# The last two of 32 expert steps behind a branch on the planned number of steps

## The chip, the cores and the metric

The kernel runs on one core of a Trainium2 chip. A core has a matmul engine (TensorE, "PE" in the profile), a vector engine (VectorE, "DVE"), an activation engine (ScalarE, "ACT"), GpSimd ("POOL") and SyncE ("SP"). Each engine works through its own list of instructions in order, and semaphores tie the lists together. DMA queues carry data between DRAM and the on-chip memory; here SP and ACT issue the plain transfers, and POOL the ones whose addresses are read from a table. The metric is device microseconds (us) of a whole execution of the kernel, as the median of several runs.

## What is computed

Two layers of a graph network over 3125 nodes of 256 features. Each layer adds a graph part and a linear attention part to `x`, and then a mixture of experts. The change touches the experts of layer 0, which in the reference are these lines (cut):

```python
N, E, D, H = 3125, 8, 256, 1024
logits = xt @ Wr + br
top_p, top_idx = jax.lax.top_k(jax.nn.softmax(logits, axis=-1), 2)
weights = top_p / top_p.sum(axis=-1, keepdims=True)
xn = (xt - mu) * jax.lax.rsqrt(var + LN_EPS)
xe = xn[None] * ln_g[:, None, :] + ln_b[:, None, :]
h = jax.nn.gelu(jnp.einsum('end,edh->enh', xe, W1) + b1[:, None, :], approximate=False)
y = jnp.einsum('enh,ehd->end', h, W2) + b2[:, None, :]
out = (weights[:, :, None] * y_of_the_two_chosen_experts).sum(axis=1)
```

Each of the 3125 tokens uses two of the 8 experts, so there are 6250 token-expert pairs; which expert gets how many depends on the data.

## The kernel before, in words

**Stages.** `fast` runs, one after the other: counting the edges and layer 0's graph and attention parts; the routing of the tokens; layer 0's experts; the projections for layer 1 (the loop over `NB` = 25 tiles of 128 nodes that begins with the gather of L2342); and layer 1 itself. `gps_two_layers` ends with a branch (L2418): if a flag is set, a slower general program follows; otherwise its code is skipped.

**Routing.** `Routes.tokens` computes the router, picks two experts per token, and scatters the normalized tokens (POOL, L1947) to the DRAM table `route_x`, where each expert has a region of 13 tiles of `TS` = 256 rows. `Routes.clear` writes zeros to all of that table beforehand, 256 rows per DMA on SP, dealt out at four DMAs per load of `at` in the loop over layer 0's node groups. `Routes.plan` counts the tiles. Every expert's first tile is always run, which makes 8 steps (`NE0`). The further tiles of expert e, max(ceil(count/256) - 1, 0) of them, are numbered through by a running sum `cum` (L1965), so that `cum[7]` is the number of further steps that the data need. There can be at most `NT` = (2 * 3125) // 256 = 24 of those, and the kernel always runs all 24. `tiles` holds expert and first row of each; the steps beyond `cum[7]` get some valid tile that nobody asked for, and what they write is read by nobody.

**Experts.** `experts` runs 8 + 24 = 32 steps. A step loads (SP) 256 rows of tokens, small vectors and the expert's two weight matrices, 1 MB each; step s loads for s + 1 ahead, with two buffers of weights. From step 8 on, SP reads expert and row from `tiles` into registers. Then for each of 8 pieces of the hidden layer: two matmuls (L2068, `fhp`) and a gelu on ACT (L2069, `fhid`); the transposes of the next step's tokens (L2051, `ftp`) and their scaling on DVE (L2053, `fxe`); 16 matmuls with W2 (L2076, `fyp`), a DVE addition (L2078, `fy`), and a store of 256 rows to the DRAM table `route_y` (ACT, L2079). Under `manual_schedule` PE, DVE and ACT keep the order in which the code is written; SP and POOL do not.

**Beside the experts.** `beside(s)` puts pieces of another job, the edge lists for layer 1 (`B_.finish`), between the steps: one piece after each step from step 8 on. After the last step it runs what is left of them, which ends with the matmuls `b_ep` (L1125), a chain of small DVE operations (L1128 to L1140) and the store `b_rows` (SP, L1141), and then the check sum `tot` (L2298).

**After the experts.** The pools of the experts' buffers are given back. SP loads layer 1's weights: `wq`, `wo` (L353, 256 KB each), `wt` (L353, 2 MB), `wkv` (L2321, twice 256 KB) and small ones. POOL gathers for every tile of nodes two tiles `y` from `route_y` (L2342), DVE adds them to `xs` (L2345) and normalizes, PE transposes (L345) and multiplies with `wt` (L2362, `hp`).

Of the kernel before, what the change touches and what calls it, by code (L numbers as in the profile page):

```python
# [10 lines left out]
I32 = mybir.dt.int32  # L11
AF = mybir.ActivationFunctionType
OP = mybir.AluOpType
AX = mybir.AxisListType
PSUM = bass.MemoryType.PSUM
# [3 lines left out]
P = 128  # L19
# [14 lines left out]
NE0, H0 = 8, 1024  # L34
# [872 lines left out]
BIG = 1e30  # L907
RW = 7
MIXED = 8
CW = 8  # L910
GB = 4
TOGETHER = [(0, 4), (4, 4), (8, 4), (12, 4), (16, 4), (20, 3), (23, 2)]
GROUPS1 = GROUPS[:5] + [(2560, 256), (2816, 256), (3072, 128)]
TS = 256
# [229 lines left out]
class Layer1:  # L1144
# [66 lines left out]
    def turn(self, A, c):  # L1211

        if c >= A["n"]:
            return
        k = min(CW, A["w"] - c * CW) * P
        ot = self.wk.tile([P, CW * P], BF, name="ot", bufs=3)
        self.nc.vector.tensor_scalar(ot[:, :k], A["oe"].pop(c)[:, :k], self.C.p, None, op0=OP.is_equal)
        A["ot"][c] = ot
# [610 lines left out]
class Routes:  # L1829


    def __init__(self, nc, C, pool, dram):
        t = lambda shape, dt, name: pool.tile(shape, dt, name=name)
        self.x = dram.tile([NE0 * XR, D], F32, name="route_x")
        self.y = dram.tile([(NE0 + NT) * TS, D], F32, name="route_y")
        self.slot = t([P, 2, NB], I32, "slot")
        self.at = t([P, 2, NB], F32, "route_at")
        self.ex = t([P, 2, NB], F32, "route_ex")
        self.more = t([P, NE0], F32, "route_more")
        self.cum = t([P, NE0], F32, "route_cum")  # L1840
        self.wt = t([P, 2, NB], F32, "route_w")
        self.start = t([P, NE0], F32, "route_start")
        nc.vector.tensor_scalar(self.start, C.row[:, :NE0], float(XR), None, op0=OP.mult)
        self.down = t([P, NE0], F32, "route_down")
        nc.vector.tensor_scalar(self.down, C.row[:, :NE0], -1.0, float(NE0), op0=OP.mult, op1=OP.add)
        self.base = t([P, NE0], F32, "route_base")
        nc.vector.tensor_copy(self.base, self.start)
        self.ones = t([P, P], F32, "route_ones")
        nc.vector.memset(self.ones, 1.0)
        self.tiles = t([1, 2, NT], I32, "route_tiles")  # L1850

    def clear(self, tc, z):

        for i in range(0, NE0 * XR, 2 * P):
            tc.keep_in_program_order(
                tc.nc.sync.dma_start(self.x[i:i + 2 * P, :].rearrange("(p a) d -> p (a d)", p=P), z))
            yield

    def tokens(self, tc, C, wk, ps, xs, t0, nt, wr, br):
# [93 lines left out]
    def plan(self, nc, C, wk):  # L1953


        t = lambda shape, name, dt=F32: wk.tile(shape, dt, name="pl_" + name, bufs=1)
        cnt = t([P, NE0], "cnt")
        nc.vector.tensor_tensor(cnt, self.base, self.start, OP.subtract)
        ci = t([P, NE0], "ci", I32)
        nc.vector.tensor_scalar(ci, cnt, float(-TS), 0.0, op0=OP.add, op1=OP.max)  # L1960
        nc.vector.tensor_single_scalar(ci, ci, TS - 1, op=OP.add)
        nc.vector.tensor_single_scalar(ci, ci, 8, op=OP.arith_shift_right)
        more, cum = self.more, self.cum
        nc.vector.tensor_copy(more, ci)
        nc.vector.tensor_tensor_scan(cum, self.ones[:, :NE0], more, 0.0, op0=OP.mult, op1=OP.add)  # L1965
        sh = [1, NT, NE0]
        le = t(sh, "le")
        nc.vector.tensor_tensor(le, cum[0:1, None, :].to_broadcast(sh),
                                C.row[0:1, :NT, None].to_broadcast(sh), OP.is_le)
        ex = t([1, NT], "ex")  # L1970
        nc.vector.tensor_reduce(ex, le, AX.X, OP.add)
        nc.vector.tensor_tensor(le, le, more[0:1, None, :].to_broadcast(sh), OP.mult)
        done = t([1, NT], "done")
        nc.vector.tensor_reduce(done, le, AX.X, OP.add)

        nc.vector.tensor_tensor(done, C.row[0:1, :NT], done, OP.subtract)
        nc.vector.tensor_scalar(done, done, 1.0, float(XR // TS - 1), op0=OP.add, op1=OP.min)
        nc.vector.tensor_scalar(ex, ex, float(NE0 - 1), None, op0=OP.min)
        nc.vector.tensor_copy(self.tiles[:, 0, :], ex)
        row = t([1, NT], "row")  # L1980
        nc.vector.tensor_scalar(row, ex, float(XR // TS), None, op0=OP.mult)
        nc.vector.tensor_tensor(row, row, done, OP.add)
        nc.vector.tensor_scalar(self.tiles[:, 1, :], row, float(TS), None, op0=OP.mult)
# [25 lines left out]
        nc.vector.tensor_copy(self.back, rank)  # L2009


def experts(tc, C, T, a, pool, wp, wk, ps, beside):

    nc = tc.nc
    K1 = H0 // P

    def fetch(s):
        if s < NE0:
            e, row = s, s * XR
            we = lambda w: w[e:e + 1]  # L2020
            col = lambda v: v[:, e:e + 1, :]
        else:
            ld = lambda i, hi: nc.values_load(
                T.tiles[0:1, i, s - NE0:s - NE0 + 1], engines=[SPE], min_val=0, max_val=hi,
                skip_runtime_bounds_check_because="a step of the plan")
            e, row = ld(0, NE0 - 1), ld(1, NE0 * XR - TS)
            we = lambda w: w[bass.ds(e, 1)]
            col = lambda v: v[:, bass.ds(e, 1), :]
        x = wk.tile([P, TS // P, D], F32, name="fx")
        rows = T.x[row:row + TS, :] if s < NE0 else T.x[bass.ds(row, TS), :]  # L2030
        nc.sync.dma_start(x, rows.rearrange("(t p) d -> p t d", p=P))
        lng, lnb = (wk.tile([P, 1, 2], F32, name=f"fln{c}") for c in "gb")
        b1 = wk.tile([P, 1, K1], F32, name="fb1")
        b2 = wk.tile([P, D], F32, name="fb2")
        nc.sync.dma_start(lng, col(a["L0_ffn_ln_gc"]))
        nc.sync.dma_start(lnb, col(a["L0_ffn_ln_bc"]))
        nc.sync.dma_start(b1, col(a["L0_ffn_b1c"]))
        nc.sync.dma_start(b2, we(a["L0_ffn_b2"]).to_broadcast([P, D]))
        w1 = wp.tile([P, 2, H0], F32, name="fw1")
        nc.sync.dma_start(w1, we(a["L0_ffn_W1"]).rearrange("e (k p) n -> p (e k) n", p=P))  # L2040
        w2 = wp.tile([P, K1, D], F32, name="fw2")
        nc.sync.dma_start(w2, we(a["L0_ffn_W2"]).rearrange("e (k p) n -> p (e k) n", p=P))
        return x, w1, w2, lng, lnb, b1, b2

    def turn(got):
        x, lng, lnb = got[0], got[3], got[4]
        xe = wk.tile([P, 2, TS], F32, name="fxe")
        tp = ps.tile([P, 2, TS], F32, name="ftp", bufs=1)
        for k in range(2):
            for t in range(TS // P):  # L2050
                nc.tensor.transpose(tp[:, k, t * P:(t + 1) * P], x[:, t, k * P:(k + 1) * P], C.id)  # L2051
        for k in range(2):
            nc.vector.tensor_scalar(xe[:, k, :], tp[:, k, :], lng[:, 0, k:k + 1], lnb[:, 0, k:k + 1],  # L2053
                                    op0=OP.mult, op1=OP.add)
        return xe

    steps = NE0 + NT
    got = [fetch(0)]
    xe = turn(got[0])
    for s in range(steps):  # L2060
        if s + 1 < steps:
            got.append(fetch(s + 1))
        x, w1, w2, lng, lnb, b1, b2 = got[s]
        hid = wk.tile([P, K1, TS], F32, name="fhid")
        for i in range(K1):
            hp = ps.tile([P, TS], F32, name="fhp")
            for k in range(2):
                nc.tensor.matmul(hp, w1[:, k, i * P:(i + 1) * P], xe[:, k, :], start=(k == 0), stop=(k == 1))  # L2068
            nc.scalar.activation(hid[:, i, :], hp, AF.Gelu, bias=b1[:, 0, i:i + 1])  # L2069
        if s + 1 < steps:  # L2070
            xe = turn(got[s + 1])
        y = wk.tile([P, TS // P, D], F32, name="fy")
        for t in range(TS // P):
            yp = ps.tile([P, D], F32, name="fyp")
            for i in range(K1):
                nc.tensor.matmul(yp, hid[:, i, t * P:(t + 1) * P], w2[:, i, :], start=(i == 0),  # L2076
                                 stop=(i == K1 - 1))
            nc.vector.tensor_tensor(y[:, t, :], yp, b2, OP.add)  # L2078
        nc.scalar.dma_start(T.y[s * TS:(s + 1) * TS, :].rearrange("(t p) d -> p t d", p=P), y)  # L2079
        beside(s)  # L2080
# [32 lines left out]
def fast(ctx: ExitStack, tc: tile.TileContext, a, out, flag):  # L2113
# [155 lines left out]
    with tc.tile_pool(name="blk", bufs=1) as blk, tc.tile_pool(name="blk_p", bufs=1, space=PSUM) as blk_p, \  # L2269
# [8 lines left out]
        def beside(s):  # L2278
# [9 lines left out]
                    next(loads, None)  # L2288
            else:
                next(steps, None)  # L2290
            if s < NE0 + NT - 1:
                return
            run_all(steps)

# [8 lines left out]
        with tc.tile_pool(name="fw", bufs=2) as fw, tc.tile_pool(name="fk", bufs=3) as fk, \  # L2303
                tc.tile_pool(name="fp", bufs=2, space=PSUM) as fp:
            with tc.manual_schedule(engines=ORDERED):
                experts(tc, C, T_, a, f, fw, fk, fp, beside)


    with tc.tile_pool(name="n1", bufs=1) as n1:
# [161 lines left out]
```

## Time and profile before

| what | us |
|---|---|
| runs shown: median (lowest to highest, 3 runs) | 3045.12 (3043.67 to 3058.38) |
| the profiled execution, its own time | 3573.77 |
| its span on the core | 3571.6 |
| PE busy in it | 2645.9 (74%) |
| DVE busy in it | 1843.1 (52%) |
| POOL busy in it | 990.8 (28%) |
| granted PE clock, mean of the span | 0.864 |
| stage of layer 0's experts (first to last matmul L2051/L2076) | 928 to 1415 |

The profiled execution is one execution under the hardware profiler; it took 529 us longer than the median of the runs shown. All positions ("at 1415") are us from the start of its span. In the rows, "PE L2076 MATMUL fyp<-fw,fhid ... x32" means line 2076, operation, tile written and tiles read, and how often. A matmul of 32-bit numbers is two instructions in the trace, so the 8 x 2 matmuls of a step's first half are 32. SPq and ACTq rows are transfers being issued, not transferred. "[10.36 <-DMA wkv...]" is the idle time of the engine before the row and what the profiler took to have ended it.

### The profile page before, as it was taken

The page shows a single profiled execution, that of the slowest core. Times are in us where ns is not written, and L with a number is a line of the kernel's source. Part 1 is how long each engine was busy: PE and PEld are TensorE (multiplying, and loading weights), DVE is VectorE, ACT ScalarE, POOL GpSimd, SP SyncE. Part 2 cuts the span into 40 slices and gives each one's busy share as a digit, 9 for nine tenths or more (in the row PEclk, how much of TensorE's full clock was granted, in tenths as well). Part 3 has the DMA queues.
Part 4 walks back from the last instruction along what each step waited for, and adds up shares of the span by engine and source line. Part 5 has one row for each costly group of instructions (what it writes and reads, how often), then busy time and mean ns, then how long its engine had stood idle before and what let it go on. Part 6 is the DMA issues. An engine that isn't in the chain of part 4 may idle for free.

```text
span 3571.6 us, 38056 instructions
## 1 busy us (share of the span) xinstructions
PE 2645.9 (74%) x13443; PEld 1791.6 (50%) x13485; DVE 1843.1 (52%) x4089; ACT 741.6 (21%) x1662; POOL 990.8 (28%) x1040
## 2 busy tenths in 40 slices
PE   3787999999699998899053557757656747756778
PEld 2555545546588887444043434534444534444456
DVE  7997977565311111866145444545545454454452
ACT  3443111222222222322001011111101111111122
POOL 1000000012360000400634553354444534544500
PEclk9999999999799999899576777778877878877889
DMA  3333565332566655533423333243333433343312
GB/s 98 81 73 88 164 211 165 99 104 74 160 201 203 196 161 175 156 126 128 128 79 83 97 110 103 81 114 104 106 98 101 117 90 92 100 121 87 107 57 84
DMA packets 388220, 421.79 MB, mean 118 GB/s; under 512 B 144181, under 2 KB 322618, under 8 KB 387764
## 3 DMA queue, kind: packets, MB, share of 16 engines
q1 hardware_dynamic: 317486, 270.75, 25.3%
q0 software_dynamic: 49072, 132.49, 13.4%
q10 hardware_dynamic: 21462, 16.03, 1.5%
q8 instruction: 108, 1.77, 0.2%
q14 instruction: 92, 0.75, 0.1%
HBM read 321.17 MB, written 97.96 MB: 117 GB/s over the span
## 4 chain that ended last, share of the span: by engine, by line
PE 50%; DVE 18%; another core or an unknown queue 17%; issue 6%; DMA 5%; ACT 3%; POOL 1%; ACTq 1%; SPq 0%; DVEq 0%; POOLq 0%
PE agg L2218 8%; PE fyp L2076 6%; PE fhp L2068 6%; PE sums L1492 6%; PE hp L1284 5%; PE hp L2362 4%; PE yp L1336 3%; DVE r L1478 2%; DVE oh_a L1656 2%; PE hp L2240 1%; DVE oh_s L1656 1%; DMA at<-adj 1%; PE kv L1764 1%; PE cnt L1671 1%
## 5 line engine op out<-in xcount | busy, mean ns | idle before, releaser
L1403 POOL DMA_INDIRECT r<-tab,b_at x831 | 795.4, 957 | 1101.5 <-ACT xt L1550 447.2
L1492 PE MATMUL sums<-r,oh 128*128 128x264 f32 x1662 | 459.3, 434 | 99.5 <-DVE oh L1481 41.3
L1492 PEld LDWEIGHTS sums<-r,oh 128*128 128x128 f32 x1662 | 355.8, 217 | 194.9 <-issue 87.9
L1228 PE MATMUL dp<-a,ot 128*128 128x64 bf16 x2493 | 118.1, 211 | 351.6 <-DVE own L1239 128.2
L1239 DVE TENSOR_TENSOR own<-dp,orel 128x512 f32<-128x512 f32 (+1 forms) x122 | 74.2, 608 | 490.6 <-remote 338.1
L1228 PEld LDWEIGHTS <-ot 128*128 128x128 bf16 x2493 | 109.2, 110 | 382.8 <-issue 202.1
L1947 POOL DMA_INDIRECT route_x<-x,slot x50 | 50.6, 1012 | 819.7 <-DVE slot L1943 646.3
L1478 DVE TENSOR_TENSOR r<-r,fixed 128x1792 f32<-128x1792 f32 (+2 forms) x123 | 239.5, 1947 | 3.4 <-ACT fixed L1466 3.4
L2068 PE MATMUL fhp<-fxe,fw 128*128 128x256 f32 x1024 | 234.0, 386 | 8.3 <-ACT fhid L2069 7.6
L1336 PE MATMUL yp<-ew,h 128*128 128x256 f32 x600 | 174.4, 443 | 85.6 <-DVE xs L1340 68.7
L1287 ACT ACTIVATE h<-hp,bc 128x512 f32<-128x512 f32 (+2 forms) x168 | 104.9, 639 | 635.5 <-remote 312.6
L2076 PE MATMUL fyp<-fw,fhid 128*128 128x256 f32 x1024 | 226.3, 379 | 0.0
L2218 PE MATMUL agg<-at,py 128*128 128x512 bf16 (+5 forms) x1181 | 215.1, 333 | 2.6 <-issue 1.8
L2218 PE MATMUL agg<-at,px 128*128 128x512 bf16 (+2 forms) x1027 | 213.9, 356 | 1.2 <-DMA row_b<-in_L_gnn_b 0.2
L2068 PEld LDWEIGHTS fhp<-fxe,fw 128*128 128x128 f32 x1024 | 186.9, 192 | 49.4 <-ACT fhid L2069 15.5
L1284 PE MATMUL hp<-xt,ew 128*128 128x512 f32 (+2 forms) x336 | 183.5, 677 | 30.0 <-ACT h L1287 24.6
L2076 PEld LDWEIGHTS fyp<-fw,fhid 128*128 128x128 f32 x1024 | 192.1, 190 | 24.8
L2362 PE MATMUL hp<-wt,xt 128*128 128x512 f32 x400 | 184.6, 610 | 11.1 <-issue 4.4
L1336 PEld LDWEIGHTS yp<-ew,h 128*128 128x128 f32 x600 | 128.7, 223 | 124.8 <-DVE xs L1340 75.1
L2069 ACT ACTIVATE fhid<-fhp,fb 128x256 f32<-128x256 f32 x256 | 120.6, 474 | 299.1 <-PE fhp L2068 221.0
L1284 PE MATMUL hp<-h,ew 128*128 128x512 f32 (+2 forms) x336 | 158.6, 599 | 0.0
L2342 POOL DMA_INDIRECT y<-route_y,slot x50 | 50.7, 1014 | 384.6 <-DMA wq<-in_L_mix_wqT 350.2
(422 smaller groups left out, 3843.7 us busy)
## 6 DMA issues: line engine op xcount, KB each, us to landing
fw<-in_L_ffn_W SPq DMA_DIRECT2D x64, 1024.0 KB
ew<-in_L_ffn_expert_w SPq DMA_DIRECT2D x126, 256.0 KB
at<-adj SPq DMA_DIRECT2D x44, 640.0 KB
route_x<-zero SPq DMA_DIRECT2D x104, 256.0 KB
tab<-stage SPq DMA_DIRECT2D x25, 1056.0 KB
oe<-b_order SPq DMA_DIRECT2D x97, 256.0 KB
adj<-adj_o SPq DMA_DIRECT2D x78, 250.0 KB
r<-tab,b_at POOLq DMA_INDIRECT x831
```

Of the source, the lines that this page charges most:

```text
L1228: nc.tensor.matmul(dp[:, i, :, :].rearrange("p h r -> p (h r)"), ot[:, i * P:(i + 1) * P], A["a3"][:, j, :], start=(j == 0), stop=(j == 2))
L1284: nc.tensor.matmul(hp[:, :W], ws[i, e][:, n, j * P:(j + 1) * P], x[:, n, :W], start=(n == 0), stop=(n == 1))
L1336: nc.tensor.matmul(yp, h2[e][:, n, i * P:(i + 1) * P], ws[3, e][:, n, :], start=(n == 0), stop=(n == 1))
L1403: st = self.nc.gpsimd.indirect_dma_start(out=r[:, c, :], out_offset=None, in_=self.table, in_offset=bass.IndirectOffsetOnAxis(ap=self.B.at ...
L1478: nc.vector.tensor_tensor(rv, rv, self.factors[:, s0:s0 + k, :, None].to_broadcast([P, k, HD, DH]), OP.mult)
L1492: mm = nc.tensor.matmul(self.sums, oh[:, c, :], r[:, c, :], start=(i == 0), stop=(i == w - 1))
L1656: nc.vector.tensor_tensor(oh.rearrange("p w (m two) -> p w m two", two=2), self.row, v[:, :, None, :].to_broadcast(self.shape), OP.is_equal)
L2068: nc.tensor.matmul(hp, w1[:, k, i * P:(i + 1) * P], xe[:, k, :], start=(k == 0), stop=(k == 1))
L2069: nc.scalar.activation(hid[:, i, :], hp, AF.Gelu, bias=b1[:, 0, i:i + 1])
L2076: nc.tensor.matmul(yp, hid[:, i, t * P:(t + 1) * P], w2[:, i, :], start=(i == 0), stop=(i == K1 - 1))
L2218: nc.tensor.matmul(agg[g][:, :cw], parts[j][:n, k, g * P:(g + 1) * P], at[:n, i, :cw], start=(k == 0 and j == 0), stop=(k == NB - 1 and j ...
L2362: nc.tensor.matmul(hp.rearrange("p r d -> p (r d)"), xt[:, k, :], wt[:, k, j * 512:(j + 1) * 512], start=(k == 0), stop=(k == 1))
```

## The change

The number of further steps, compared with 22, is kept on the chip as `over`. The first 30 steps run as before; the last two run inside `tc.If(over > 0)`, as a call of `experts` of its own with its own buffers, which loads the first of its two steps itself. The rest of `beside`'s job, which was run after step 31, is run after step 29. Since the rows of `route_y` that steps 30 and 31 would write may now stay unwritten, `clear` writes zeros to them too. In the diff, line numbers count lines of the file before and after.

```diff
+SELDOM = 2
@@ class Routes
+        self.over = t([1, 1], I32, "route_over")
@@ def clear
-        for i in range(0, NE0 * XR, 2 * P):
+        pieces = [(self.x, i) for i in range(0, NE0 * XR, 2 * P)]
+        pieces += [(self.y, i * TS) for i in range(NE0 + NT - SELDOM, NE0 + NT)]
+        for x, i in pieces:
             tc.keep_in_program_order(
-                tc.nc.sync.dma_start(self.x[i:i + 2 * P, :].rearrange("(p a) d -> p (a d)", p=P), z))
+                tc.nc.sync.dma_start(x[i:i + 2 * P, :].rearrange("(p a) d -> p (a d)", p=P), z))
@@ def plan
         nc.vector.tensor_tensor_scan(cum, self.ones[:, :NE0], more, 0.0, op0=OP.mult, op1=OP.add)
+        nc.vector.tensor_single_scalar(self.over, cum[0:1, NE0 - 1:], float(NT - SELDOM), op=OP.is_gt)
@@ def experts
-def experts(tc, C, T, a, pool, wp, wk, ps, beside):
+def experts(tc, C, T, a, pool, wp, wk, ps, beside, first, steps):
-    steps = NE0 + NT
-    got = [fetch(0)]
-    xe = turn(got[0])
-    for s in range(steps):
+    got = {first: fetch(first)}
+    xe = turn(got[first])
+    for s in range(first, steps):
@@ def fast: beside
-            if s < NE0 + NT - 1:
+            if s < NE0 + NT - SELDOM - 1:
                 return
             run_all(steps)
@@ def fast
-                experts(tc, C, T_, a, f, fw, fk, fp, beside)
+                experts(tc, C, T_, a, f, fw, fk, fp, beside, 0, NE0 + NT - SELDOM)
+        with tc.If(nc.values_load(T_.over[0:1, 0:1], min_val=0, max_val=1) > 0):
+            with tc.tile_pool(name="fw_l", bufs=2) as fw, tc.tile_pool(name="fk_l", bufs=3) as fk, \
+                    tc.tile_pool(name="fp_l", bufs=2, space=PSUM) as fp:
+                with tc.manual_schedule(engines=ORDERED):
+                    experts(tc, C, T_, a, f, fw, fk, fp, lambda s: None, NE0 + NT - SELDOM, NE0 + NT)
```

## Prediction, written before the result

> **What bounds the kernel now.** I read three views, from coarse to fine. First the busy times by stretch: the experts' stage, then the gap behind it, then layer 1's projections. (Columns: stretch, length, busy time and count of PE, PE weight load, DVE, ACT, POOL, granted clock, DMA share, GB/s.)
>
> ```profile
> 1330.00:1415.00 85.00, 85.00 (x404) 72.45 (x402) 12.62 (x40) 22.78 (x48) 0.00 (x0) 1.00 0.55 161
> 1415.00:1435.00 20.00, 1.36 (x9) 0.86 (x8) 7.27 (x26) 2.54 (x6) 11.54 (x12) 0.57 0.76 256
> 1435.00:1515.00 80.00, 71.38 (x189) 33.75 (x190) 66.42 (x203) 23.34 (x67) 39.17 (x38) 0.89 0.53 163
> ```
>
> In the last steps PE is busy 85.00 of 85.00 us at granted clock 1.00: each us of matmul there is a us of the kernel. In the next 20 us PE does next to nothing. So two prices are wanted: of two steps, and of the gap. For both, the chain that ended last (start, length, what):
>
> ```profile
> 1386.68 0.22 PE b_ep L1125 x2
> 1386.90 6.93 PE fhp L2068 x32
> 1393.82 0.44 PE ftp L2051 x4
> 1394.26 6.91 PE fyp L2076 x32
> 1401.17 6.96 PE fhp L2068 x32
> 1408.13 6.92 PE fyp L2076 x32
> 1415.08 0.42 DVE fy L2078
> ...
> 1417.45 9.40 DMA wkv<-in_L_mix_wkT
> 1426.85 0.49 DVE xs L2345
> ```
>
> Steps 30 and 31 follow each other on PE without a hole; then the chain leaves PE for transfers. The timeline of the gap:
>
> ```profile
> 1403.94 0.32 SPq L1141 DMA_DIRECT2D b_rows<-b_add  x1
> 1415.53 0.37 ACTq L2079 DMA_DIRECT2D route_y<-fy  x1
> 1415.94 0.38 SPq L353 DMA_DIRECT2D wq<-in_L_mix_wqT  x1
> 1418.50 1.02 POOL L2342 DMA_INDIRECT y<-route_y,slot  x1 [350.16 <-DMA wq<-in_L_mix_wqT]
> 1426.85 0.48 DVE L2345 SCALAR_TENSOR_TENSOR xs<-y,route_w,xs 128x256 f32<-128x256 f32 x1 [10.36 <-DMA wkv<-in_L_mix_wkT]
> 1433.82 1.09 PE L345 MATMUL tp<-ident,x 128*128 128x128 f32 x4 [17.91 <-DVE x L338]
> 1435.06 8.79 PE L2362 MATMUL hp<-wt,xt 128*128 128x512 f32 x16
> ```
>
> The gather names `wq` as what it waited for, but it reads `route_y`: the last store, issued until 1415.90, is its likely cause, so a 256 KB store lands within 2.6 us. Likewise the first `xs` needs the gathers, not `wkv`: they were issued 2.6 us behind 3 MB of weights and share the DMA engines with them. POOL idled 350 us before; nothing runs past this gap, so whatever the stage saves arrives at the end.
>
> **Is the branch taken?** No row tells. I ran the reference's routing on its own inputs: the experts get 779, 1053, 1364, 1084, 120, 330, 1129 and 391 tokens, so 3+4+5+4+0+1+4+1 = 22 further steps. 22 > 22 is false: the steps are skipped. It would need 122 more tokens on one expert (391 to 513) to make it 23; rounding can't do that.
>
> **What goes.** By the chain, from 1386.68 to 1415.05: 0.22 + 14.28 + 13.88 = 28.4 us. Step 29 also loses the transposes for step 30, 0.44 us on PE. Of the 28.4, `b_ep` (0.22) only moves behind step 29. With T0 as the end of the last `fyp`, T0 comes **28.8 us earlier**. ACT's 16 gelus, four `fy`, and the loads of two steps on SP (4 MB of weights) go with it and gain nothing: they ran under PE.
>
> **What comes, early.** `over` is one DVE operation of about 0.17 us (as its neighbour L1965) in the plan at 918; the next matmul waits for `fx` until 928, so nothing. SP reads `over` ahead of the first `fx` load (in the changed program it stands just before it); that load waited for the scatters until 925.27, seven us after `over` is there: nothing; without that cover about 0.5 us. The two zeroings of `route_y` are two more SP issues of 0.6 us and 512 KB at about 600, at the end of layer 0's graph part, where the `at` loads run four buffers ahead and PE waits for none: nothing, at most 1.2 us.
>
> **What comes, at the branch.** Every engine reads `over`, compares and jumps. The rows show SP reading registers in the steps: between `fw` at 1358.10 (0.38 long) and `fx` at 1359.00 one read cost 0.52 us; between `fx` and `flng` (1360.35) 0.98. I take 0.5 for the three engines with work there; they read side by side. The skipped stretch costs something too: the changed program has, for the path not taken, a place where SP waits for all transfers on the eight hardware DMA semaphores before it counts on. Queued behind it are the `wq` to `wkv` loads, and POOL's first gather, which needs those counts. Times from T0:
>
> - before: `fy` done +0.45, `wq` issued +0.9, first gather +3.45, first `xs` +11.8, first `hp` +20.0.
> - after: the job beside ends here, uncovered: DVE's chain from `b_et` to `b_add` (1401.55 to 1403.65 in the trace, 2.1 us) follows `fy`, to +2.6; `b_rows` is issued +2.9 to +3.2 (0.29 behind, as in the trace) and lands 2.6 later at most: +5.8. Then the gather, +6.1 instead of +3.45. SP also reads the other flag now before `wq` (0.5 to 1.0): +6.9 instead of +0.9.
>
> So the gather is 2.65 us late and the weights 6.0. But the gathers now stand ahead of the weights. Unhindered, the first lands at 6.1 + 0.95 + 2.6 = +9.7, and by the trace 7.0 us of DVE and 1.2 of transposes follow: `hp` could start at +17.9. It needs `wt` as well: 2.5 MB up to `wt`, with 0.8 MB of gathers in between, at the 0.36 MB/us of that stretch, is 9.1 us: about +18 with the latency. The bounds: 2.1 us gained (+17.9), or 6.0 lost (all of SP's delay on the path, +26). The weights were just in time before, the gathers late; nearest to that row is no great change. I take +21, a loss of **1.0 us**.
>
> **A rule against the change.** "Runtime: NRT & Kernel Launch", section Instruction fetch mechanics, says a taken branch breaks the sequential prefetch, and that a target outside the window held on chip stalls the engine for a fetch. It gives no price. The skipped body is 272 instructions on PE (136 matmuls, each with a weight load) but some 33 on SP, 18 on ACT, 8 on DVE, none on POOL. The nearest row is the branch at the kernel's end over the whole general program: the last output is issued until 3565.69, the span ends at 3571.6, so that jump, the last write and the closing cost 5.9 us together. By the row at its worst, a stall on SP would put `wq` at +12.8 and `hp` up to +32: 12 lost. By the rule read closely, only PE's jump is long, and PE has 17.9 us of idleness to hide it. I take nothing and keep the 12 as a rival.
>
> **After the branch.** The order of instructions differs a little in the first and last of the 25 projection tiles: DVE and ACT operations of neighbouring tiles swapped. That stage keeps PE 71 and DVE 66 of 80 us; I allow 3 us either way and take nothing.
>
> **Sum.** 3573.8 - 28.8 + 1.0 = 3546.0 for the profiled execution. It took 529 us more than the median, and nothing shows where. The steps are matmuls back to back at full granted clock, which an ordinary run cannot shorten, so I subtract the same 27.8: 3045.1 - 27.8 = **3017.3 us**.
>
> **Rivals.**
> - The branch is dear (12 lost as above): gain 16.8, 3028. For it: the whole gap hangs on SP's list. Against: its jump is short.
> - Ordinary runs spend less on the steps, by the ratio 3045/3574: gain 24.5 - 1.0, 3021.6. For it: the unexplained 529 us. Against: clock 1.00 and PE without a hole.
> - Slower: the branch is taken, deciding from a count of 23. Then step 30's loads start only at +3.2 instead of a step ahead: six issues with register reads (about 0.6 each) up to `w1`, 1.4 MB at 0.36 MB/us is 3.9, 2.6 of latency, and 1.7 of transposes and scaling: the first `fhp` at about +13.5 instead of at once, plus 0.5 for the reads: 3059. For it: the count sits on the very edge. Against: the 122 tokens.
>
> **Numbers.** Likeliest case 0.76, dear branch 0.10, cheaper steps 0.08, taken 0.04, the rest unforeseen. The likeliest case's own ends are gains of 28.8 + 2.1 + 3 = 33.9 and 28.8 - 6.0 - 3 = 19.8. The runs before scatter from -1.5 to +13 about their median, so I take 3009 to 3029. 0.5% of 3045 is 15.2 us, about what a measurement can tell from no change: faster means below 3029.9. Faster 0.88 (all of the first and third case and some of the dear branch), same 0.07, slower 0.05.
>
> **What would show it.** Right: 960 `fhp` and `fyp` matmuls instead of 1024, 30 stores of `route_y`, 60 loads of `fw`; the last `fyp` ending near 1386.2; `b_rows` some 3 us later; the first gather near 1392.3, the first `hp` near 1407; a span near 3544. Wrong: 1024 `fhp` with a hole of 13 us in them (taken); the first gather more than 9 us behind the last `fyp` (SP's wait or a fetch); a projection stage longer than 80 us by more than 3.

## The result and the profile after

| | us |
|---|---|
| before, median (lowest to highest, 5 runs) | 3057.8 (3043.7 to 3059.7) |
| after, median (lowest to highest, 5 runs) | 3027.1 (3005.5 to 3033.0) |
| after / before, 95% interval | 0.9899 (0.9876 to 0.9921) |
| the gain by that ratio, of 3057.8 | 30.9 (24 to 38) |
| span of after's profiled execution | 3025.3 |

The changed kernel is faster by 1.0%, with an interval that leaves out 1; the forecast was 3017.3, its range 3009 to 3029, its gain 27.8. The three runs of before that the prediction started from had a median of 3045.1; with two more it is 3057.8.

Lines of the changed kernel are those of its own file: `fhp` L2068 is now L2072, `ftp` L2051 L2056, `fyp` L2076 L2080, `b_ep` L1125 L1126, `b_rows` L1141 L1142, `wkv` L2321 L2330, the gather L2342 L2351, `xs` L2345 L2354, `hp` L2362 L2371; the branch is L2311.

Groups and DMA issues on the page of the changed kernel:

```profile
L2072 PE MATMUL fhp<-fxe,fw 128*128 128x256 f32 x960 | 219.5, 387 | 0.9 <-DVE fxe L2058 0.6
L2080 PE MATMUL fyp<-fw,fhid 128*128 128x256 f32 x960 | 212.2, 379 | 0.0
...
fw<-in_L_ffn_W SPq DMA_DIRECT2D x60, 1024.0 KB
```

960 instead of 1024, 60 instead of 64: two steps are gone, so the branch was not taken. Ahead of all the matmuls of these two groups together PE stood idle for 0.9 us (1.1 in an ordinary execution of before, the run base below): the other steps lost nothing there.

Its timeline from step 28's second half to the first `hp` (start, length, what; in brackets the engine's idle time and what ended it):

```profile
1343.54 7.12 PE L2072 MATMUL fhp<-fxe,fw 128*128 128x256 f32 x32
...
1350.94 7.07 PE L2080 MATMUL fyp<-fw,fhid 128*128 128x256 f32 x32
1357.85 7.12 PE L2072 MATMUL fhp<-fxe,fw 128*128 128x256 f32 x32
1364.80 7.07 PE L2080 MATMUL fyp<-fw,fhid 128*128 128x256 f32 x32
1371.71 0.38 PE L1126 MATMUL b_ep<-ident,b_ends 128*25 128x128 f32 x2
...
1374.64 0.32 SPq L1142 DMA_DIRECT2D b_rows<-b_add  x1
...
1376.44 0.27 DVE L2339 MEMSET pad<- 1x256 f32 x1 [1.07 <-SPq L2311]
...
1377.63 1.01 POOL L2351 DMA_INDIRECT y<-route_y,slot  x1 [325.31 <-DVE pad L2340]
1378.02 0.39 SPq L353 DMA_DIRECT2D wq<-in_L_mix_wqT  x1
...
1381.59 0.48 DVE L2354 SCALAR_TENSOR_TENSOR xs<-y,route_w,xs 128x256 f32<-128x256 f32 x1 [4.86 <-DMA y<-route_y,slot]
...
1392.93 1.09 PE L345 MATMUL tp<-ident,x 128*128 128x128 f32 x4 [17.91 <-DMA kb<-in_L_mix_ln_k_b]
...
1394.10 1.22 PE L2379 MATMUL ap<-score_w,xt 128*128 128x128 f32 x4
...
1396.38 0.66 PE L345 MATMUL tp<-ident,x 128*128 128x128 f32 x2 [1.06 <-DVE mv_x L2357]
...
1396.83 9.05 PE L2371 MATMUL hp<-wt,xt 128*128 128x512 f32 x16
```

A step is still 14.31 us (1343.54 to 1357.85). The last `fyp` ends at 1371.87 (1364.80 + 7.07); that point is T0 from here on. From there to the first `hp` it is 24.96 us, where before it was 20.02. Of these 4.9 us, 2.3 are a later first transpose (`tp` at +21.1, where before it was at +18.8). The other 2.7 come from PE's order, which changed too: before, the first tile's `tp` is followed at once by its `hp`; here the scheduler put the first tile's score matmuls (`ap`, which before stand behind `hp`) and half of the second tile's transposes in between. In the gap the job's tail is now uncovered: `b_ep`, the chain to `b_add`, `b_rows` at +2.8. The gather follows at +5.8, and `wq` at +6.2, behind the gather, where it was ahead of it.

The chain that ended last cannot be followed back past 1376 in this trace, so of the steps it says nothing. In the gap it names what `hp` waits for (start, length, what):

```profile
1378.95 0.99 POOL y L2351
1379.93 0.30 issue
1380.24 7.15 DMA y<-route_y,slot
1387.39 0.02 issue
1387.41 0.49 DVE xs L2354
1387.90 0.10 DVE mv_x L2357
1388.00 0.17 issue
1388.17 6.84 DMA y<-route_y,slot
```

It is gathers now (7.15 and 6.84 us each from issue to use), not the weights. The last of them is for a later tile, but its `xs` stands on DVE ahead of the last operations for the second tile, whose transposes PE does ahead of `hp`.

### The profile page after: what moved, and what is told of

Read it like the earlier page. It is cut to its first block, busy times and chain, and to the rows that moved or that the text cites. A ratio compares the mean times of both kernels' runs of the same rounds, so it can differ in the third digit from the quotient of the medians.

```text
span 3025.3 us, 37763 instructions
## 1 busy us (share of the span) xinstructions
PE 2522.7 (83%) x13349; PEld 1720.9 (57%) x13349; DVE 1842.2 (61%) x4082; ACT 735.1 (24%) x1646; POOL 997.2 (33%) x1040
## 3 DMA queue, kind: packets, MB, share of 16 engines
q0 software_dynamic: 49072, 132.49, 15.5%
## 4 chain that ended last, share of the span: by engine, by line
PE 29%; DVE 9%; POOL 6%; DMA 5%; issue 4%; ACT 2%; DVEq 0%; ACTq 0%; SPq 0%; POOLq 0%
PE sums L1493 8%; PE hp L1285 7%; POOL r L1404 6%; PE hp L2371 5%; PE yp L1337 4%; DMA r<-tab,b_at 3%; DVE r L1479 1%; PE kvp L2389 1%; DVE oh L1482 1%; PE dp L1229 1%; PE yp L1596 1%; DMA y<-route_y,slot 1%; DMA ew<-in_L_ffn_expert_w 1%; DVE xs L1341 1%; ACT h L1288 0%
## 5 line engine op out<-in xcount | busy, mean ns | idle before, releaser
L1493 PE MATMUL sums<-r,oh 128*128 128x264 f32 x1662 | 417.5, 407 | 46.6 <-DVE oh L1482 24.2
L1493 PEld LDWEIGHTS sums<-r,oh 128*128 128x128 f32 x1662 | 330.0, 201 | 127.4 <-issue 30.3
L2072 PE MATMUL fhp<-fxe,fw 128*128 128x256 f32 x960 | 219.5, 387 | 0.9 <-DVE fxe L2058 0.6
L1337 PE MATMUL yp<-ew,h 128*128 128x256 f32 x600 | 162.3, 422 | 66.8 <-DVE xs L1341 59.7
L2222 PE MATMUL agg<-at,py 128*128 128x512 bf16 (+4 forms) x1200 | 217.9, 335 | 0.0
L2080 PE MATMUL fyp<-fw,fhid 128*128 128x256 f32 x960 | 212.2, 379 | 0.0
L2072 PEld LDWEIGHTS fhp<-fxe,fw 128*128 128x128 f32 x960 | 176.3, 193 | 38.6 <-ACT fhid L2073 6.6
L2080 PEld LDWEIGHTS fyp<-fw,fhid 128*128 128x128 f32 x960 | 180.3, 190 | 23.2
L1285 PE MATMUL hp<-xt,ew 128*128 128x512 f32 (+2 forms) x336 | 166.7, 624 | 22.1 <-ACT h L1288 13.0
L2371 PE MATMUL hp<-wt,xt 128*128 128x512 f32 x400 | 180.7, 601 | 3.2 <-ACT xt L346 2.7
L2351 POOL DMA_INDIRECT y<-route_y,slot x50 | 51.2, 1025 | 350.4 <-DVE pad L2340 325.3
L2222 PEld LDWEIGHTS <-py 128*128 128x128 bf16 (+1 forms) x1200 | 111.5, 99 | 88.1 <-issue 5.5
L2222 PEld LDWEIGHTS <-px 128*128 128x128 bf16 (+1 forms) x1050 | 96.3, 98 | 105.4 <-issue 10.3
```

Source lines behind the costliest of these rows:

```text
L1285: nc.tensor.matmul(hp[:, :W], ws[i, e][:, n, j * P:(j + 1) * P], x[:, n, :W], start=(n == 0), stop=(n == 1))
L1337: nc.tensor.matmul(yp, h2[e][:, n, i * P:(i + 1) * P], ws[3, e][:, n, :], start=(n == 0), stop=(n == 1))
L1493: mm = nc.tensor.matmul(self.sums, oh[:, c, :], r[:, c, :], start=(i == 0), stop=(i == w - 1))
L2222: nc.tensor.matmul(agg[g][:, :cw], parts[j][:n, k, g * P:(g + 1) * P], at[:n, i, :cw], start=(k == 0 and j == 0), stop=(k == NB - 1 and j ...
L2371: nc.tensor.matmul(hp.rearrange("p r d -> p (r d)"), xt[:, k, :], wt[:, k, j * 512:(j + 1) * 512], start=(k == 0), stop=(k == 1))
```

## The experiments

Two theories stood against each other on what the branch costs: that the skipped code is as good as free and the longer gap comes from `b_rows` and what waits for it, or that the branch itself (the reads, the wait ahead of it, the jump) is what holds the gap. Beside these: what the gap is worth at all, since a longer one cost nothing that the total shows. Times are medians; the ratio is to before, run in between on the same chip (before's medians there: 3057.3 for base, only30, taken and early_job, 3055.6 for two_branches and the three with preload). All marks are us after T0.

### base: the kernel before, once more

No edit. It shows how far two sets of runs of one kernel lie apart, and whether the profiled execution of 3571.6 us was a typical one.

> The kernel before, unchanged, once more, for a profile of an ordinary execution: the first one took 529 us more than the median. Every theory expects a ratio of 1.000. If those 529 us were a matter of that one execution, the span is now near 3055, the expert steps are still 14.3 us each, and the gap from the last fyp to the first hp is still 20 us. If they came with the profiler, the span is again near 3570.

Measured: 3059.5 (22 runs), ratio 1.0007 (0.9993 to 1.0020), profiled span 3064.1. So the 500 us belonged to that one execution. From its last `kv` matmul (1705.1) to its end it took 1866 us; here, from 1686.7, 1377: 489 us of the surplus were in layer 1. Of the 18 us ahead of that matmul, 10 were in the experts, where steps 2 to 8 took 15.3 to 16.1 us each. The steps of this ordinary execution, by the timeline of PE:

```profile
1374.92 7.09 PE L2068 MATMUL fhp<-fxe,fw 128*128 128x256 f32 x32
...
1382.28 7.07 PE L2076 MATMUL fyp<-fw,fhid 128*128 128x256 f32 x32
1389.19 7.12 PE L2068 MATMUL fhp<-fxe,fw 128*128 128x256 f32 x32
```

14.27 us from one `fhp` to the next, as in the last steps of the long execution and in after. The stage of the experts (first `ftp` to T0) is 476.9 us here and 451.5 in after: 25.4 less, against 28.8 by the chain. The missing 3.4 us are nearly all in steps 22 and 23, which share PE with other work: they took 45.4 us in after and 42.1 here. In the six kernels that run 30 steps the stage lies between 447.9 and 451.5.

### only30: the two steps left out without a branch

Leaves out steps 30 and 31 whatever the count is, so it computes what is asked only while the data need at most 22 further steps.

```diff
-        with tc.If(nc.values_load(T_.over[0:1, 0:1], min_val=0, max_val=1) > 0):
-            ...
-                    experts(tc, C, T_, a, f, fw, fk, fp, lambda s: None, NE0 + NT - SELDOM, NE0 + NT)
```

> The changed kernel without its branch: the last two steps are left out, never to be run. Theory A (the branch costs little by itself; the gap grew because SP, which stands at the branch until b_rows has landed, holds back the first gather and the weights): wq is issued at +3.3 after the last fyp instead of +6.2, the first gather at about +3.5 instead of +5.8, hp at about +22 instead of +25, so about 3 us less than with the branch. Rival B (the branch costs much more than the trace of its gap shows, through something later in the program): 10 us or more less than with the branch. Rival C (the gain comes partly from elsewhere than the two steps): the two steps alone give clearly less or more than 28.8 us against the kernel before.

Measured: 3029.4 (6 runs), ratio 0.9908 (0.9875 to 0.9941): not to be told from after. Its timeline in the gap (T0 1380.05):

```profile
1382.82 0.32 SPq L1142 DMA_DIRECT2D b_rows<-b_add  x1
...
1384.63 0.27 DVE L2334 MEMSET pad<- 1x256 f32 x1 [1.24 <-DMA b_rows<-b_add]
1384.72 0.37 SPq L353 DMA_DIRECT2D wq<-in_L_mix_wqT  x1
...
1385.76 1.02 POOL L2346 DMA_INDIRECT y<-route_y,slot  x1 [323.58 <-DVE pad L2335]
```

The gather was expected at +3.5 and comes at +5.7. From `b_rows` to the gather it is 2.94 us here and 2.99 in after: the gather waits for that store with or without a branch. Only `wq` comes sooner without it, by 1.5 us (+4.7 against +6.2), and `hp` gains nothing from that (+25.98 against +24.96): the weights now go out ahead of the first gather, and the first `xs` is at +13.3 instead of +9.7.

### taken: the same branch, taken

Computes everything; only the count from which the branch is taken is one lower.

```diff
-        nc.vector.tensor_single_scalar(self.over, cum[0:1, NE0 - 1:], float(NT - SELDOM), op=OP.is_gt)
+        nc.vector.tensor_single_scalar(self.over, cum[0:1, NE0 - 1:], float(NT - SELDOM - 1), op=OP.is_gt)
```

> The changed kernel with the threshold at 21 instead of 22, so that with 22 further steps the branch is taken and all 32 steps run. By the prediction the first fhp of step 30 comes 13.5 us after step 29's last fyp, and the time is 14 us above the kernel before (ratio 1.0045). If the jump and a fetch of the body are dear, the hole is 16 us or more; if SP can load ahead of the branch, it is under 5.

Measured: 3069.7 (14 runs), ratio 1.0042 (1.0025 to 1.0058), which is 12.8 us (7.6 to 17.7) slower than before. The timeline of PE:

```profile
1383.66 0.19 PE L2303 MATMUL tot<-ok,b_found 128*1 128x1 f32 x2
1387.75 1.09 PE L2056 MATMUL ftp<-ident,fx 128*128 128x128 f32 x4 [3.90 <-DMA fx<-route_x]
1394.35 9.06 PE L2072 MATMUL fhp<-fxe,fw 128*128 128x256 f32 x32 [5.52 <-DMA fw<-in_L_ffn_W]
```

The hole ends with the load of 1 MB of `fw`, which could not be issued ahead of the branch. From step 29's last `fyp` (to 1380.70) to `fhp` it is 13.7 us, and the time shows about as much. This is the price when the data need 23 or 24 further steps.

### two_branches: one branch for each step

Both are skipped; so a second branch is added and each skips half.

```diff
+        self.over2 = t([1, 1], I32, "route_over2")
...
+        nc.vector.tensor_single_scalar(self.over2, cum[0:1, NE0 - 1:], float(NT - 1), op=OP.is_gt)
...
-                    experts(tc, C, T_, a, f, fw, fk, fp, lambda s: None, NE0 + NT - SELDOM, NE0 + NT)
+                    experts(tc, C, T_, a, f, fw, fk, fp, lambda s: None, NE0 + NT - 2, NE0 + NT - 1)
+        with tc.If(nc.values_load(T_.over2[0:1, 0:1], min_val=0, max_val=1) > 0):
+            ...
+                    experts(tc, C, T_, a, f, fw, fk, fp, lambda s: None, NE0 + NT - 1, NE0 + NT)
```

> The changed kernel with step 30 and step 31 each behind a branch of its own (more than 22, more than 23), one after the other; neither is taken. Theory A (a branch that is not taken costs SP a register read and little else once nothing is in flight; what it really costs is the wait for transfers in flight): the first gather comes at most 1 us later than the +5.8 of the changed kernel, wq at +7 to +7.5, and the time is the same within what can be measured. Rival B (each branch costs a jump and a fetch of its own): gather at +8 or later, hp at +27 or later.

Measured: 3029.4 (5 runs), ratio 0.9924 (0.9895 to 0.9954). The gather comes at +6.65 instead of +5.76 and `wq` at +7.36 instead of +6.15: a second branch costs 0.9 to 1.2 us at the two places, as theory A expected, and nothing that the time shows.

### early_job: the job's tail back under the matmuls

Computes everything. Two more pieces of the job run beside step 20, so that `b_rows` is done before the steps end and nothing of the tail stands in the gap.

```diff
+            if s == 20:
+                next(steps, None)
+                next(steps, None)
```

> The changed kernel with two more pieces of the job beside done after step 20, so that b_ep, its DVE chain and b_rows are over before step 29 ends. Theory A: SP at the branch now waits only for the last route_y store (issued until +0.9, landing by +3.5), so the first gather goes at about +3.5 instead of +5.8, wq at +3.9 instead of +6.2, and hp comes 2 us earlier than +25. Rival B (the branch itself, its register reads and its jump, makes the delay): gather and wq stay at +5.8 and +6.2, less at most 0.5.

Measured: 3033.8 (7 runs), ratio 0.9933 (0.9910 to 0.9956): no gain; 4 to 7 us slower than only30 and after by the medians, though the intervals overlap. Its timeline (T0 1368.72):

```profile
1369.62 0.38 SPq L353 DMA_DIRECT2D wq<-in_L_mix_wqT  x1
1370.05 0.50 SPq L353 DMA_DIRECT2D wo<-in_L_mix_woT  x1
1370.60 0.47 SPq L353 DMA_DIRECT2D wt<-in_L_gnn_WT  x1
1381.53 0.38 SPq L2333 DMA_DIRECT2D wkv<-in_L_mix_wkT  x1
...
1382.36 1.02 POOL L2354 DMA_INDIRECT y<-route_y,slot  x1 [330.12 <-SPq L2314]
```

The weights do come at +0.9. But with nothing left to wait for, the scheduler put `wq`, `wo` and `wt` ahead of the branch on SP, and then SP issues nothing for 10.5 us, and the gather, expected at +3.5, starts at +13.6. The program has SP wait on the skipped path until all transfers on the hardware queues have landed, and 2.5 MB had just been issued. The trace shows these waits (engine and line, what it waited for, us in total, times, longest):

```profile
SPq L2314 <- SPq L2314: 9.9, 4, 6.5
```

The jump itself is over at 1371.18. The longest wait ends at 1381.19, and it is for the semaphore on which `wt` reports that it has landed. The first `hp` is at +26.8, and the 25th tile's `kvp` is 7.2 us later after T0 than in after (280.2 against 273.0).

So the wait at the branch is real. In after it is 1.1 us by the same view, because only `b_rows` and the last `route_y` are in flight there.

### preload_after, preload_before, preload_early: the weights loaded during the steps

`wq`, `wo`, `wt` and `wkv` are loaded beside step 24, into buffers of their own, in after, in before and in early_job.

```diff
+    n1 = ctx.enter_context(tc.tile_pool(name="n1", bufs=1))
+    r0 = pre.enter_context(tc.tile_pool(name="r0", bufs=1))
...
+            if s == 24:
+                W1["wq"] = load_k(nc, n1, a["L1_mix_wqT"], "wq")
+                W1["wo"] = load_k(nc, n1, a["L1_mix_woT"], "wo")
+                W1["wt"] = load_k(nc, r0, a["L1_gnn_WT"], "wt")
+                W1["wkv"] = wkv = r0.tile([P, 2, 2 * D], F32, name="wkv")
+                ...
```

> The changed kernel with wq, wo, wt and wkv (3 MB) loaded during steps 24 to 29, into room of their own, so that none of them is asked for behind the branch. Theory A: the first gather still waits for b_rows, at +5.8, but the first gathers no longer share the DMA engines with 3 MB of weights: first xs at +9.5, hp at +17 to +18 instead of +25. Question of the catching up: in the changed kernel the 5 us of later hp were made up by the third tile. If PE's start sets the stage's end, the 25th tile is 7 us earlier than +273; if the gathers and DVE set it, it is within 3 us of +273.

> The kernel before, with the same preloading and no branch. It tells whether preloading helps by itself: gather at +3.5, first xs at +7.1, hp at +15 instead of +20, so 5 us less than before if PE's start sets the end of the projections (ratio 0.998), nothing if it does not.

> preload_after, with the job beside finished two steps earlier as well, so that at the branch only the last route_y store and small vectors are in flight. Theory A: gather at +3.6 to +5, first xs at +7.3 to +9, hp at +15 to +17. By the same two answers of the catching up the 25th tile comes 8 us earlier than in the changed kernel (3018 us where the changed kernel has 3027), or within 3 us of it (3024 to 3030).

| | median (runs) | ratio (95%) |
|---|---|---|
| preload_before | 3056.0 (22) | 1.0009 (0.9994 to 1.0024) |
| preload_after | 3030.4 (7) | 0.9926 (0.9900 to 0.9952) |
| preload_early | 3036.9 (10) | 0.9946 (0.9926 to 0.9966) |

Loading ahead brought PE's first `tp` 4.0 us forward in after and 3.3 in before, and neither kernel is measurably faster by it: of the 5 us expected in preload_before, its interval leaves at most 1.8. preload_early was expected to have its gather at +3.6 to +5 and `hp` by +17; they came at +8.8 and +21.8. There the scheduler put the loads of `bo`, `kg` and `kb` ahead of the branch, and SP waited 4.3 us for them.

What PE runs into behind its start is seen in preload_after:

```profile
1395.69 9.06 PE L2376 MATMUL hp<-wt,xt 128*128 128x512 f32 x16
...
1409.38 3.70 PE L2376 MATMUL hp<-wt,xt 128*128 128x512 f32 x8 [0.75 <-DVE stage L2379]
1416.89 3.78 PE L2376 MATMUL hp<-wt,xt 128*128 128x512 f32 x4 [3.81 <-DVE stage L2379]
```

and on DVE at the same place:

```profile
1412.71 0.42 DVE L2361 BATCH_NORM_STATS2 st_x<-xs 128x6 f32<-128x256 f32 x1
1415.09 0.48 DVE L2359 SCALAR_TENSOR_TENSOR xs<-y,route_w,xs 128x256 f32<-128x256 f32 x1 [1.96 <-DMA y<-route_y,slot]
1415.49 0.17 DVE L2362 BATCH_NORM_AGGREGATE mv_x<-st_x 128x2 f32<-128x6 f32 x1
1415.58 0.65 DVE L2404 TENSOR_REDUCE var<-sq 128x8 f32<-128x512 f32 x1
1416.15 0.68 DVE L2379 COPY stage<-hp 128x512 f32<-128x512 f32 x1
```

PE's second tile cannot go on until DVE has emptied its result into `stage`; DVE takes its work in order, and an `xs` of a later tile stands ahead of that copy and waits for its gather. The wait costs twice: the four `hp` behind it take 3.78 us, where four at full clock take 1.98. The ten us from 40 us after T0 on, in preload_after and then in after (stretch, length, busy times of PE, PE weight load, DVE, ACT, POOL, then PE's granted clock, of which 1.00 is full speed):

```profile
1417.43:1427.43 10.00, 9.76 (x26) 4.85 (x25) 7.68 (x24) 2.57 (x8) 4.99 (x4) 0.73 0.62 191
...
1411.87:1421.87 10.00, 10.00 (x31) 4.76 (x29) 8.83 (x30) 3.19 (x9) 7.53 (x8) 1.00 0.71 224
```

In the four kernels in which one such wait lasted 3.8 to 4.7 us (base and the three with preload) the granted clock of these ten us is 0.66 to 0.83; in the other five, where none was longer than 2.6, it is 1.00.

All nine, in two groups by PE's order in the first tiles, one profile each (us after T0):

| | first `tp` | first `hp` | idle on `stage` | idle in all | lost to the clock | 25th `kvp` |
|---|---|---|---|---|---|---|
| before's order: | | | | | | |
| base | 18.8 | 20.2 | 4.8 | 25.1 | 3.4 | 274.9 |
| preload_before | 15.5 | 16.7 | 5.3 | 22.1 | 4.8 | 273.6 |
| preload_after | 17.1 | 18.3 | 5.0 | 23.3 | 5.1 | 275.4 |
| preload_early | 20.6 | 21.8 | 5.0 | 26.9 | 5.3 | 279.0 |
| early_job | 25.7 | 26.8 | 3.0 | 30.0 | 3.1 | 280.2 |
| `ap` and half of the next `tp` first: | | | | | | |
| after | 21.1 | 25.0 | 0.5 | 23.7 | 3.4 | 273.0 |
| only30 | 23.3 | 26.0 | 1.8 | 27.4 | 2.2 | 275.8 |
| two_branches | 22.6 | 25.5 | 1.4 | 25.7 | 2.8 | 274.9 |
| taken | 19.4 | 22.1 | 2.8 | 24.2 | 2.7 | 272.7 |

"Idle on `stage`" is PE's idle time before `hp` in the first 110 us behind T0 that the groups put down to the copies into `stage`. "Idle in all" is PE's over the first 160 us; "lost to the clock" is an estimate: PE's busy time in each us of these 160, times what the granted clock lacked to 1 there. Taken off the last column, the two leave 245.8 to 247.1 in every row, so they account for where the stage ends. In after against preload_after, PE starts 4.0 us later, but it waits 4.5 less on `stage` and loses 1.7 less to the clock.

What spares after the wait is not settled. It isn't the later start alone: preload_early starts later than base and waits as long, and early_job, the latest of all, still waits 3.0. The four that wait least are those with the changed order, which came with the other changes; no run changes the order alone. Within one order, a later start mostly does put off the end (15.5 to 25.7 against 273.6 to 280.2, and 19.4 to 23.3 against 272.7 to 275.8), though with one profile each some us may be scatter.

No version tried is faster than after.

## Why the prediction was right

**The branch is skipped**: right, by the counts.

**The two steps are worth 28.8 us, the same in an ordinary execution**: right. The step is 14.3 us in the long execution, in base and in after alike, and leaving two out without a branch gives 28 us (18 to 38; 1 - 0.9908 of 3057.3). The rival that ordinary runs spend less on the steps falls with that. Its footing, the surplus of 529 us, lay in layer 1 but for some 18 us.

**What comes early costs nothing**: the first `ftp` is at 920 to 931 in all of the runs, with no order between those that have the new operation, read and zeroings and those that don't. A cost below some us would not be seen in that.

**The gap**: the positions came out, one reason did not.

| us after T0 | predicted | measured |
|---|---|---|
| `b_rows` issued | 2.9 | 2.8 |
| first gather | 6.1 | 5.8 |
| `wq` issued | 6.9 | 6.2 |
| first `xs` | 9.7 | 9.7 |
| first `hp` | 21 (17.9 to 26) | 25.0 |

The gather was put down both to the landing of `b_rows` and to SP's wait at the branch, whose counts POOL needs. only30 has no such wait and the same delay: the store alone makes it. And the first `hp` is near the late bound for a reason that the prediction left out. The gathers, now ahead of the weights, still took 7 us each, which put the first `tp` at +21.1; with 1.2 us of transposes, `hp` at +21 would have needed it at +19.8. The larger part of the delay, 2.7 us, is PE's changed order; the prediction had seen only DVE and ACT operations swapped.

**"A loss of 1.0 us" for the gap**: the term was built wrongly, though small. It took each us of PE's later start as a us of the end. The end also depends on what PE then waits for and at which clock it runs: in after against base, PE's idle time over the first 160 us is 1.4 us less, although its start is later. By the 25th tile's `kvp` the loss was -1.9 us in after, 0.0 in two_branches and +0.9 in only30, so about nothing; in early_job, with before's order, it was 5.3. That after loses nothing is luck as far as the prediction goes: it foresaw neither the order nor these waits.

**The rule on instruction fetch and the rival of 12 us lost**: no stall of that size. The trace of after has the branch on each engine (engine, operation, count, duration in ns, start); cut to PE and SP:

```profile
L2311 SPq EVENT_SEMAPHORE  x9: 17/17/17, 1375.2 to 1376.7; - x9
L2311 SPq TENSOR_LOAD <-route_over x1: 466/466/466, 910.4 to 910.4; - x1
...
L2311 SPq COMPARE_BRANCH  x1: 53/53/53, 1375.0 to 1375.0; - x1
...
L2311 PEldq COMPARE_BRANCH  x1: 352/352/352, 1375.4 to 1375.4; - x1
L2311 PEldq EVENT_SEMAPHORE  x1: 51/51/51, 1375.8 to 1375.8; - x1
```

PE's jump over 272 instructions takes 0.35 us, those of the other engines 0.05 to 0.08, and PE's next instruction follows at once; in two_branches, where each branch skips half, PE's second jump takes 0.22. So the longest jump is the dearest here, but by a third of a us, in a gap where PE waits anyway. SP had read `over` long before, at 910; what it spends at the branch, 1.7 us from the jump on, is a row of nine waits, 1.1 us of it real waiting. Without the branch `wq` comes 1.5 us sooner (only30), and a second branch adds 0.9 to 1.2; the time of neither shows it.

**The rival that the branch is taken**: it didn't occur, but the run that forced it gave the price that was worked out for it: 12.8 us (7.6 to 17.7) against 14 (3059 - 3045), and a hole of 13.7 in place of 13.5. The parts that the prediction lists for the hole add up to 15.0, though; the 13.5 holds if the 1.7 of transposes and scaling are hidden, and the run shows that: `ftp` is at 1387.75, 6.6 us ahead of `fhp`, which waits for `fw`.

**The sum**: 27.8 forecast, 30.9 (24 to 38) measured. That the time itself came out 9.8 above the forecast has its cause in the other term: 3045.1 as the time before, a median of three runs that scatter by 15. On 3057.8 the same subtraction gives 3030.0, 2.9 above what was measured. The gain was right; that 3027.1 lies 1.9 inside the range owes something to the range, which allowed for that scatter.

## What to carry to other kernels

Steps that fill PE back to back can be priced from the chain of waits, and that price holds even in an execution whose total is far from the usual; what comes behind a stage has to be followed beyond PE's first instruction: the order in which the scheduler puts the next work, a wait further on, and the clock behind that wait can outweigh a start some us earlier or later. Ahead of a branch, look at what is in flight on the engines that must wait there: leaving a small store uncovered in front of it was harmless, moving big loads ahead of it held the gathers for 10 us. And a branch that is skipped for nothing costs its whole start-up when it is taken: here about 13 us lost against about 30 gained, by the data.

## What the runs showed that was not expected

A single profiled execution took 3571.6 us where 22 runs of the same kernel lay between 3039 and 3073, with 489 us of its surplus in layer 1. And a kernel's runs scatter by some 15 us about their median on this one core, half of what this change brings. In the nine ordinary profiles, layer 1, which the change doesn't touch, takes 1362 to 1377 us, so much of that scatter can come from there. Three runs are too few for the level; a gain of this size needs runs of both kernels on the same occasion.
